# Requesting rows of delta * x eight units ahead of their use instead of ten

## The chip, the cores and the metric

The kernel runs as one program on 1 core of a Trainium2 chip. The metric is the device time of one execution in microseconds (us), given as a median over runs.

## The reference, cut to what matters

Four layers run one after another on images with 128 channels. Layers 0 and 1 each contain a selective scan over 4 batches, in four directions over 64 x 64 = 4096 positions; layer 0 has 128 channels there and layer 1 has 256. For every channel there are 16 states, and each is a first-order recurrence along the positions:

```python
def step(h, inp):
    d, u, b, c = inp
    dA = jnp.exp(d[..., None] * A)
    h = dA * h + (d * u)[..., None] * b[:, :, None, :]
    y = jnp.sum(h * c[:, :, None, :], axis=-1)
    return (h, y)
```

`d` is delta (a softplus of a projection), `u` the image x after a convolution, `b` and `c` are projections of x that all channels share. Around the scans stand 1x1 and 3x3 convolutions, norms and gates. Layer 2 is a message passing over 3x3 neighbours, layer 3 an attention over 7x7 windows; the change does not touch them.

## The kernel before

**Tiling.** The scans of layers 0 and 1 are 12 tasks: 4 batches with one tile of 128 channels for layer 0 and with two for layer 1. A task has 16 steps (4 directions, each in 4 pieces of 1024 positions), and a step has 16 units. A unit is 8 channels times 16 states on the 128 partitions, by 1024 positions. There are 3072 units, taken in pairs.

**A unit's way.** `prepare` computes for a whole step delta, delta * x and the projections. It stores delta * x to a DRAM tile `dud` (line 417, three of these tiles), cuts delta into three bfloat16 parts `parts`, copies these in 12 pieces of 64 KB into a tile `dp` (line 428), and asks for the rows of C, each repeated over 8 partitions, as `repC` (line 387). `load` (line 445) then requests for a unit its 8 rows of delta * x, each repeated over 16 partitions: 512 KB from `dud` into half of a pair tile `h` (line 453). There are nine pair tiles. VectorE multiplies the pair by B in place (`times`, line 459). TensorE spreads delta over the states and ScalarE takes the exponential (`decay`, lines 467 and 469) in one of two PSUM tiles `da`. VectorE runs the recurrence along the positions (`scan`, line 478), again in place. GpSimd (POOL) multiplies the pair by C (`times`, line 459), and TensorE adds up the states into `yps` (`add_up`, line 559). After that the pair tile can be filled again.

**Order.** The order is written by hand. `Scans.run` (line 587) goes through slots u, one per unit. In slot u VectorE gets the scan of unit u, in every other slot followed by the multiply by B of the next pair, TensorE the decay of unit u + 2 and, in odd slots, the sum of the pair whose last unit is u - 6. All DMAs of the scans are issued by SyncE (SP), in the order in which the program lists them; an entry that waits holds up all behind it. Tile frees and landings are told by semaphores, and eight of these serve the DMAs in turn, so that a DMA also waits for the eighth before it to land.

**What shares SyncE's queue.** `Plan.post` keeps a store or a load back until a due time that a planner computes, and `Plan.flush` issues it at the start of a later slot. Where u + 28 is a multiple of 16 (slot 4 of every step), line 628 issues all that is left of the preparing chains "prep" and "rep" and starts the preparation of another step; for a second channel tile this reads `xd` back (line 380). When `load` comes to the first unit of a step it flushes the chain "prep" (line 448). `between` hands out pieces of the other work of layers 0 and 1 ("side work": convolutions, norms, output projections), with loads such as `pad` (line 806), `x` (line 784) and `big` (line 1088) and stores (line 760). At the very end of a slot stands

```python
if 0 <= u + LEAD < total:
    self.load(u + LEAD)
```

so that all entries of slot u come before the request of unit u + LEAD.

Of the kernel before, what the change touches and what calls it, by code (L numbers as in the profile page):

```python
# [280 lines left out]
NU = ND * NSTEP * NG  # L281
FULL = 3600
AHEAD = 28
LEAD = 10
LAG = 5


class Scans:
# [298 lines left out]
    def run(self, between, head):  # L587
# [9 lines left out]
        for u in range(-12, total + LAG + 1):  # L597
# [52 lines left out]
            self.fill(self.plan.cells)  # L650
            if 0 <= u + LEAD < total:
                self.load(u + LEAD)
        while self.later:
# [1328 lines left out]
class Attention:  # L1982


    NH, HD, LEAD = 4, 32, 2

# [217 lines left out]
    def run(self):  # L2204
# [7 lines left out]
        def chunk_of(m):  # L2212
            return divmod(m, NCH)

        for m in range(self.LEAD):
            for piece in self.project(*chunk_of(m)):
# [6 lines left out]
        for n in range(total + 4):  # L2223
            if n % 4 == 0 and n < total:
                assert not pieces
                m = n // 4 + self.LEAD
                self.load(*chunk_of(m + 2))
# [243 lines left out]
```

## Time and profile before

| what | value |
|---|---|
| median of 3 runs | 12899.53 us (12898.79 to 12918.31) |
| the profiled execution, its own time | 12904.32 us |
| its span, first to last instruction | 12902.2 us |
| VectorE (DVE) busy | 11778.0 us, 91% |
| GpSimd (POOL) busy | 9663.1 us, 75% |
| TensorE (PE) busy | 9366.9 us, 73% |
| ScalarE (ACT) busy | 7769.0 us, 60% |
| requests of delta * x (`h<-dud`) | 3072 of 512 KB |
| bytes moved by DMA | 2463.66 MB, 191 GB/s over the span |
| scans, from about 112 us to 10,991 us | then layers 2 and 3 |

In the profile a line names the kernel's line (L478), the engine and operation, the tiles as output<-inputs, then busy time and the mean of one instruction in ns, then the idle time of the engine just before, and what ended it. In a timeline the first column is the start, the second the duration, and brackets hold the idle time before. In the list of waits stand the waiting engine and line, what it waited for, the total in us, how often, and the longest. "SPq" is SyncE's queue: its entries there are DMA issues, not the transfers themselves, which land later.

### The profile page before, as it was taken

To read this page: it belongs to the slowest core of one execution; us is meant where nothing else is said; L and a number is where in the kernel's file an instruction comes from. 1 tells how busy PE (TensorE), PEld (TensorE's weight loads), DVE (VectorE), ACT (ScalarE), POOL (GpSimd) and SP (SyncE) were. 2 spreads that over 40 slices of the span, in tenths; PEclk is the share of its full clock that TensorE was granted. 3 is DMA by queue.
4 is the path that set the end of the run, shared out by engine and by line. 5 is a ranking of instruction groups with operands and counts; after the bars stand their busy time and mean duration, and the time that the engine had idled before them with its cause. 6 is when DMAs were issued, how large, how long until landed. Compare 5 with 4: busy or idle time off the path is not lost. (4 is left out here: it accounts for less than half of the span.)

```text
span 12902.2 us, 128082 instructions
## 1 busy us (share of the span) xinstructions
PE 9366.9 (73%) x40881; PEld 2741.6 (21%) x41435; DVE 11778.0 (91%) x7219; ACT 7769.0 (60%) x10392; POOL 9663.1 (75%) x3167
## 2 busy tenths in 40 slices
PE   6777777767767767667777677776777776776799
PEld 1111111111111111111111111211112121221455
DVE  7999999999999989998999999999999999498666
ACT  4666656655666546655666555555555555476576
POOL 6888888887888778887888788888888888266200
PEclk8888899889889888998999899989899889887899
DMA  6888888898888978898888987778878777255200
GB/s 177 213 221 233 223 213 225 213 233 216 211 222 208 218 192 212 217 230 215 213 218 216 220 217 201 208 199 200 218 193 200 206 195 188 69 144 134 68 21 17
DMA packets 873450, 2463.66 MB, mean 191 GB/s; under 512 B 141888, under 2 KB 163528, under 8 KB 865096
## 3 DMA queue, kind: packets, MB, share of 16 engines
q1 hardware_dynamic: 872775, 2455.44, 74.3%
q8 instruction: 330, 5.41, 0.2%
q14 instruction: 345, 2.82, 0.1%
HBM read 2035.79 MB, written 268.17 MB: 179 GB/s over the span
## 5 line engine op out<-in xcount | busy, mean ns | idle before, releaser
L459 POOL TENSOR_TENSOR h<-h,repC 128x2048 f32<-128x2048 f32 x1536 | 6953.9, 4533 | 1476.3 <-ACT state L496 1176.7
L478 DVE TENSOR_TENSOR_SCAN h<-da,state,h 128x1024 f32<-128x1024 f32 x2304 | 5294.1, 2338 | 281.5 <-ACT da L469 168.1
L469 ACT ACTIVATE da<-da,av 128x1024 f32<-128x1024 f32 x3072 | 3327.5, 1087 | 2912.7 <-PE da L467 2486.2
L467 PE MATMUL da<-dp,spread 128*128 128x512 bf16 x5802 | 1995.7, 424 | 2441.2 <-DVE h L478 2398.5
L459 DVE TENSOR_TENSOR h<-h,B 128x2048 f32<-128x2048 f32 x1536 | 3476.6, 2263 | 173.1 <-issue 80.7
L559 PE MATMUL yps<-h,gather 128*32 128x512 f32 x12288 | 1866.7, 683 | 19.2 <-issue 4.5
L478 DVE TENSOR_TENSOR_SCAN h<-da,h 128x1024 f32<-128x1024 f32 x768 | 1719.4, 2278 | 66.0 <-ACT da L469 27.2
L467 PEld LDWEIGHTS <-spread 128*128 128x128 bf16 x6144 | 588.9, 101 | 4511.5 <-issue 4115.0
L565 PE MATMUL yps<-ones,nothing 128*128 128x512 bf16 x4197 | 1235.9, 404 | 37.3 <-issue 33.8
L102 ACT ACT_TABLE_LOAD x580 | 744.1, 1283 | 11.7 <-DMA x<-in_x_dram 1.7
L102 ACT CAST parts<-delta 128x1024 bf16<-128x1024 f32 x384 | 400.7, 1043 | 555.6 <-POOL delta L102 521.3
L102 POOL TENSOR_TENSOR delta<-delta,low 128x1024 f32<-128x1024 f32 x192 | 451.6, 2352 | 271.1 <-ACT low L102 220.4
L565 PEld LDWEIGHTS <-nothing 128*128 128x128 bf16 x4409 | 382.7, 101 | 1221.9 <-issue 929.4
L2175 POOL COPY wide_total<-total 128x128 f32<-128x128 f32 x128 | 37.4, 293 | 781.3 <-DVE total L2173 214.7
L102 PE MATMUL ms<-d,wts 128*128 128x512 f32 (+3 forms) x832 | 481.6, 691 | 164.5 <-POOL d L102 58.3
L102 PE MATMUL ms<-xd,xpdt 64*128 64x512 f32 x768 | 476.5, 703 | 107.4 <-ACT delta L102 25.3
L102 POOL TENSOR_TENSOR low<-delta,xc 128x1024 f32<-128x1024 f32 x192 | 502.9, 2619 | 9.1
L2144 ACT ACTIVATE s<-s,least 128x512 f32<-128x512 f32 x512 | 368.4, 720 | 232.6 <-DVE least L2131 228.7
L542 PE MATMUL yps<-y,ident 128*128 128x512 f32 x576 | 498.6, 955 | 4.3 <-ACT y L577 1.2
L1801 POOL TENSOR_TENSOR acc<-acc,part 128x1024 f32<-128x1024 f32 x120 | 301.9, 2519 | 195.7 <-DVE part L1795 195.7
L102 ACT ACTIVATE low<-ms,av 128x512 f32<-128x512 f32 x384 | 263.7, 687 | 287.7 <-PE ms L102 258.9
L102 POOL TENSOR_TENSOR parts<-delta,parts 128x1024 bf16<-128x1024 f32 x192 | 409.5, 2133 | 31.9 <-ACT parts L102 21.6
(295 smaller groups left out, 11050.8 us busy)
## 6 DMA issues: line engine op xcount, KB each, us to landing
h<-dud SPq DMA_DIRECT2D x3072, 512.0 KB
dp<-parts SPq DMA_DIRECT2D x2304, 64.0 KB
repC<-xdd SPq DMA_DIRECT2D x192, 512.0 KB
dud<-low SPq DMA_DIRECT2D x192, 512.0 KB
spread<-gd SPq DMA_DIRECT2D x72, 1024.0 KB
pad<-xid SPq DMA_DIRECT2D x176, 256.0 KB
x<-x SPq DMA_DIRECT2D x104, 256.0 KB
yd<-y SPq DMA_DIRECT2D x96, 256.0 KB
```

The lines of the kernel that those rows point to most:

```text
L102: return call(*args, **kw)
L459: engine.tensor_mul(pair, pair, t.prepared[step][name].unsqueeze(1).to_broadcast([P, 2, TS]))
L467: self.nc.tensor.matmul(da[:, cols], self.C.spread[:, jj, :], dp[:, j, cols], start=True, stop=True)
L469: self.nc.scalar.activation(da, da, AF.Exp, scale=t.W.a[:, at : at + 1])
L478: nc.vector.tensor_tensor_scan(h[:, way], da[:, way], h[:, way], 0.0 if step % NSTEP == 0 else t.states[step - 1][:, u % NG : u % NG + 1], ...
L542: self.nc.tensor.matmul(self.like_part(yps, k), self.C.ident, self.part(t.y, k, c, b), start=True, stop=False)
L559: self.nc.tensor.matmul(out, self.C.gather[jj], rhs, start=False, stop=jj == 3)
L565: self.nc.tensor.matmul(self.live["yps"], self.C.nothing, self.C.ones16, start=False, stop=False, skip_group_check=True)
L1801: (nc.vector if alone and pair else nc.gpsimd).tensor_add(acc, acc, part)
L2144: self.nc.scalar.activation(s, s, AF.Exp, scale=-1.0, bias=self.live["least", n][:, h : h + 1], accum_out=self.live["total", n][:, h : h + 1],
L2175: nc.gpsimd.tensor_copy(wide, total.unsqueeze(2).to_broadcast([P, self.NH, self.HD]))
```

## The change

One constant is altered: the request of unit x is listed at the end of slot x - 8 instead of slot x - 10. The nine pair tiles, all instructions and all other constants stay as they are. The first request moves from slot -10 to slot -8. Every entry of SyncE's queue that is not such a request moves ahead of two of them. The flush on line 448 takes place in slot 8 of a step instead of slot 6.

```diff
 FULL = 3600
 AHEAD = 28
-LEAD = 10
+LEAD = 8
 LAG = 5
```

## The prediction

> **What bounds the kernel now.** I read the head and the slices of the page first, then its costliest groups.
>
> ```profile
> PE 9366.9 (73%) x40881; PEld 2741.6 (21%) x41435; DVE 11778.0 (91%) x7219; ACT 7769.0 (60%) x10392; POOL 9663.1 (75%) x3167
> DVE  7999999999999989998999999999999999498666
> ...
> L478 DVE TENSOR_TENSOR_SCAN h<-da,state,h 128x1024 f32<-128x1024 f32 x2304 | 5294.1, 2338 | 281.5 <-ACT da L469 168.1
> L459 DVE TENSOR_TENSOR h<-h,B 128x2048 f32<-128x2048 f32 x1536 | 3476.6, 2263 | 173.1 <-issue 80.7
> ...
> L478 DVE TENSOR_TENSOR_SCAN h<-da,h 128x1024 f32<-128x1024 f32 x768 | 1719.4, 2278 | 66.0 <-ACT da L469 27.2
> ```
>
> VectorE is busy in nine tenths or more of nearly every slice up to about 11,000 us: that stretch is the scans, and there each pair of units costs it one multiply by B and two scans. Two starts of that multiply are 6.87 us apart at the median, so a unit takes 3.44 us. Nothing in the change shortens an instruction of VectorE. What can move is its idle time, 281.5 + 173.1 + 66.0 = 520.5 us in these three groups, and new idle time of the same kind.
>
> The change touches SyncE's queue, so next its own waits and two stretches of its timeline, an easy one and a crowded one.
>
> ```profile
> SPq L453 <- PE yps L559: 3154.9, 801, 19.7
> SPq L417 <- POOL low L102: 522.9, 135, 8.1
> SPq L453 <- DMA h<-dud: 403.4, 281, 3.7
> SPq L428 <- DMA h<-dud: 299.2, 239, 2.7
> ```
> ```profile
> 9553.07 0.51 SPq L387 DMA_DIRECT2D repC<-xdd  x1
> 9553.63 9.06 SPq L428 DMA_DIRECT2D dp<-parts  x12
> 9562.86 1.20 SPq L453 DMA_DIRECT2D h<-dud  x2
> ```
> ```profile
> 2954.61 13.41 SPq L428 DMA_DIRECT2D dp<-parts  x10
> ...
> 2972.63 3.51 SPq L806 DMA_DIRECT2D pad<-ld  x4
> 2976.18 7.21 SPq L453 DMA_DIRECT2D h<-dud  x4
> ```
> ```profile
> 2978.62 4.59 DVE L478 TENSOR_TENSOR_SCAN h<-da,state,h 128x1024 f32<-128x1024 f32 x2
> 2994.29 2.29 DVE L459 TENSOR_TENSOR h<-h,B 128x2048 f32<-128x2048 f32 x1 [11.07 <-issue]
> ```
>
> First: in the scans SyncE mostly waits for TensorE to let go of an old pair (`yps` is the sum that reads it last). Second: once per step a burst of small transfers stands between two requests. Third and fourth: where side work puts four `pad` loads into the same place, the request issued at 2976.18 landed at 2994.21 by its landing mark, and VectorE stood still for 11.07 us. The line says "issue"; the landing 0.08 us before the start says what it was.
>
> **The change part by part.**
>
> *Removed and added instructions: none.* 3072 requests, nine pairs, all other work stay. The sum holds moves only.
>
> *When the tiles come free: no change.* A pair is free once the sum over the pair nine before it has been issued, in slot x - 11 for an even unit x, and that is 10 units before VectorE wants it. In the trace the request follows this release by 0.1 us at the median for units 4, 6, 8, 10 and 12 of a step, issued about 32 us before the multiply that reads it. With a lead of ten the request's place in the queue (slot x - 10) is right behind its release; with eight it is two slots later. Where nothing else is queued in these two slots, SyncE still waits for the same release, and nothing moves: cost 0, covered by that wait. If the cover were gone, it would be two slots, 6.87 us, per request.
>
> *What is moved: every other entry now goes ahead of two more requests.* The heaviest case is the burst in slot 4 of each step, all of it there because line 628 flushes it: 12 `dp` parts, `repC`, and `xd` for the second channel tile. It stood between units 13 and 14; it will stand between 11 and 12. The burst lasts 13.6 us at the median (9.5 to 18.3 from the 10th to the 90th percentile), mostly waiting for POOL and for the eighth transfer before it. Its end is 9.9 us after the release of unit 14, hence some 17 us after that of unit 12. So units 12 and 13, now asked for 32.5 and 31.4 us ahead, will be asked for about 22.5 - 6.9 = 16 us ahead, units 14 and 15 directly behind them.
>
> *Is 16 us enough?* I took, for each request, issue, last landing mark and the start of the multiply that reads it. Landing takes 7.5 us at the median, 14.9 at the 95th percentile, over 15 in 148 cases of 3072. Here the Trainium skill has a rule, "SBUF — State Buffer", section "The DMA setup-cost knee": about 2 us fixed plus the bytes over 436 GB/s. That would be an estimated 3.2 us for these 512 KB, and 16 us would be plenty: cost 0. The trace disagrees: the fastest request takes 4.2 us, requests in a full queue land 2.1 us apart, and with eight outstanding one waits for seven before it. I use the trace.
>
> The margin between landing and use is 21.4 us at the median of all requests, 17.6 and 14.9 for units 14 and 15. A usual step therefore stays covered: units 12 and 13 keep about 9 us. The tail does not. Taking the smallest margin of each step from its pair 14-15 to pair 12-13 of the next step, 18 of 191 are under 2.9 us, 24 under 5 and 34 under 6.9, bunched where side work loads `pad` tiles.
>
> *The price of a late step.* The first request behind an entry is needed 6.87 us earlier than its counterpart now. Against that, two requests of 2.1 us no longer lie ahead of it: in a saturated queue the margin shrinks by 6.87 - 4.1 = 2.8 us. Where SyncE instead waits for the burst's sources and nothing is gained but two issues of 0.6 us, it shrinks by 5.7; by all of 6.87 where not even that. Summing (shrinkage - margin) over the steps below it gives 43 us at 2.9, 64 at 4, 86 at 5 and 140 at 6.9. The steps that are late at present are saturated ones, the others nearer the middle: I take 4.5, so about +75 us. Of that cost 11 steps pay on top of what they stall now. Behind a late multiply stand the pair's two scans on VectorE, and behind these TensorE's next decays (both PSUM tiles are taken) and POOL's multiply by C; all shift together, so a stall is paid once and not again downstream.
>
> *What gets better.* Entries other than requests come up to two slots earlier. Following VectorE's longest idle times back, seven go to such transfers and not to a request: loads of `x` (6.2 and 21.8 us), of `xpdt` (12.7), `big` (9.6) and `pad` (8.5 and 12.2), and a store of `dud` that held up ACT (15.0); 86 us in all. Two requests fewer ahead are 4 us each, -28 us; at most 6.87 each, -48. At least 0, where what is late was issued late for its own source.
>
> *Order of the `xdd` stores.* `load` flushes the preparing chain when it reaches a step's first unit: slot 6 now, slot 8 then. 150 such stores stand in slot 6. Two slots more let ACT finish `xd` first (SyncE waited 85.5 us there, 29 times). Their reader, `repC`, comes most of a step later. I take 0; the ends are -10 (fewer blocked requests) and +5 us.
>
> *The head.* The first request comes in slot -8 instead of -10, behind the same `dud` store. VectorE's first multiply waited for B on TensorE, with its request landed 3 us before: 0 to +5 us; I take 0.
>
> Sum: +75 - 28 = +47 us. The profiled execution took 12904.3 us around its span of 12902.2, 5 us above the median of 12899.5; its trace is used for differences only. 12899.5 + 47 = 12946.5, said as 12947.
>
> **The rivals.**
>
> *Hidden anyway.* SyncE's main wait is for free tiles, and the usual margin is over 14 us. If late steps and earlier side loads cancel (each about 45 us), the time stays at 12,880 to 12,920. Against it: the margins of 24 steps are under 5 us. Chance 0.16.
>
> *Faster.* The wait of 3154.9 us holds everything behind it, and a lead of eight lets side loads and stores pass. If the seven idle times shrink by 6.87 us each and late steps lose only 2.8, partly taken up by the idle time that follows them anyway, it is -48 and some +20: 12,870. It decides if the side transfers gain more than the requests lose. For it: 86 us hang on such transfers, only 29 us at present on late requests. Against it: side work is planned with its own landing times and rarely ends a wait of VectorE, while a request is waited for directly. Chance 0.14.
>
> *Late in many steps.* If the burst ends no earlier and four requests back to back land as slowly as now under load, steps with a pair 14-15 margin below 10 us count: 42 of 192, 219 us, less 28: 13,090. For it: the median 17 us after release. Against it: the median landing of 7.5 us. Chance 0.08.
>
> **How the numbers follow.** My forecast has 0.62, centred on 12947. A measurement of this kernel can tell about 0.2%, 26 us, from no change. Slower by more: 0.62 + 0.08 = 0.70; within: 0.16; faster: 0.14. The range goes from 12,865 (gains at their upper end) to 13,050 (shrinkage of 6.9 and some more), leaving about 0.2 outside. The likeliest case alone spans 12,920 to 13,020.
>
> **What would show it.** Right: three VectorE groups of the same length as before with idle time of the B multiply up from 173 to some 220 to 260 us, at multiplies of units 12 to 15 of a step with the landing just before the start; SyncE's wait for `yps` smaller than 3155 us; units 12 and 13 asked for some 16 us ahead. Wrong: idle time of the B multiply unchanged; or the scans' idle behind ACT down by more than the multiply's is up; or late requests spread over all units.

## The result: 12971.5 us, half a percent slower, and the profile after

| | before | after |
|---|---|---|
| median | 12899.16 us | 12971.52 us |
| ratio, 95% interval | | 1.005 [1.0038, 1.0062] |
| profiled execution | 12904.32 us | 12970.43 us |
| span | 12902.2 us | 12968.6 us |

A second set of runs of the changed kernel gave a ratio of 1.0054 [1.0041, 1.0066]. The change costs 66 to 72 us; 47 were forecast. The lines of the page that answer to those of before:

```profile
PE 9501.4 (73%) x41435; PEld 2751.4 (21%) x41435; DVE 11778.0 (91%) x7219; ACT 7772.9 (60%) x10392; POOL 9665.4 (75%) x3167
...
L478 DVE TENSOR_TENSOR_SCAN h<-da,state,h 128x1024 f32<-128x1024 f32 x2304 | 5293.1, 2337 | 267.0 <-ACT da L469 152.8
L459 DVE TENSOR_TENSOR h<-h,B 128x2048 f32<-128x2048 f32 x1536 | 3474.6, 2262 | 265.1 <-DMA h<-dud 110.3
L478 DVE TENSOR_TENSOR_SCAN h<-da,h 128x1024 f32<-128x1024 f32 x768 | 1719.1, 2278 | 56.8 <-ACT da L469 18.0
```

VectorE's busy time is the same to a tenth of a microsecond, and the means of these three instructions agree within 2 ns. What moved are the numbers behind the second bar, the idle times: the multiply by B waits 92.0 us more (173.1 to 265.1), and the main releaser is now a request, `DMA h<-dud`. The scans wait 23.7 us less. Together that is +68.3 us, against +66.4 us in the span. (TensorE's larger busy time is no extra work: 554 of its matmuls were missing from the first trace.)

SyncE's own waits for `repC`'s place, before the change:

```profile
SPq L387 <- POOL h L459: 187.5, 104, 4.5
```

After it, with two more:

```profile
SPq L453 <- PE yps L559: 1154.5, 347, 18.3
SPq L417 <- POOL low L102: 1008.3, 143, 11.8
SPq L387 <- POOL h L459: 688.7, 132, 10.9
```

The wait for a free pair tile fell from 3154.9 to 1154.5 us: the requests' place in the queue now binds more often than their tile. What SyncE gained it spends one entry further on: on POOL for `dud` (522.9 before) and on POOL for `repC` (187.5 before, 688.7 after), which heads the burst. So the burst did not come earlier. It began 4.1 us before the start of the scan of unit 4 at the median of the steps, and now begins 4.3 us before it; it ended 9.2 us after, and now 8.9. The requests, in turn, are issued nearer to their use at every unit of a step: the median margin between landing and use fell from 21.4 to 15.4 us, and the median landing time rose from 7.5 to 9.3 us.

The crowded stretch of the prediction, in the timelines of SyncE and VectorE after the change (start, duration, instruction, idle time before):

```profile
2955.88 15.04 SPq L428 DMA_DIRECT2D dp<-parts  x11
...
2975.49 3.49 SPq L806 DMA_DIRECT2D pad<-ld  x4
2979.02 4.63 SPq L453 DMA_DIRECT2D h<-dud  x3
```
```profile
2980.09 4.59 DVE L478 TENSOR_TENSOR_SCAN h<-da,state,h 128x1024 f32<-128x1024 f32 x2
2997.32 2.29 DVE L459 TENSOR_TENSOR h<-h,B 128x2048 f32<-128x2048 f32 x1 [12.64 <-issue]
```

The same block and the same four `pad` loads, the same kind of wait: 11.07 us became 12.64. But it was the multiply of units 14 and 15 before, and it is that of 12 and 13 now, one pair earlier. The page again says "issue"; the landing mark lies 0.08 us before the start.

A finer cut than any line gives: I count an idle time before a multiply by B as *late* where one of its two requests landed less than 0.3 us before it began. All tables below use this.

| idle time in us | late, all | at 12-13 | at 14-15 | at 0-11 | other, before B | before the scans |
|---|---|---|---|---|---|---|
| before | 28.6 | 0 | 27.6 | 0.9 | 144.6 | 347.4 |
| after | 140.8 | 87.7 | 31.7 | 21.5 | 124.3 | 323.8 |

Pairs whose request landed that late rose from 11 to 41 of 1536; before four of the 41 VectorE had no idle time.

### The profile page after: what moved, and what is told of

It reads as the page before. It is cut to its first block, busy times and chain, and to the rows that moved or that the text cites. A ratio compares the mean times of both kernels' runs of the same rounds, so it can differ in the third digit from the quotient of the medians.

```text
span 12968.6 us, 128662 instructions
## 1 busy us (share of the span) xinstructions
PE 9501.4 (73%) x41435; PEld 2751.4 (21%) x41435; DVE 11778.0 (91%) x7219; ACT 7772.9 (60%) x10392; POOL 9665.4 (75%) x3167
## 5 line engine op out<-in xcount | busy, mean ns | idle before, releaser
L467 PE MATMUL da<-dp,spread 128*128 128x512 bf16 x6144 | 2091.2, 426 | 2517.9 <-DVE h L478 2487.2
L459 DVE TENSOR_TENSOR h<-h,B 128x2048 f32<-128x2048 f32 x1536 | 3474.6, 2262 | 265.1 <-DMA h<-dud 110.3
L565 PE MATMUL yps<-ones,nothing 128*128 128x512 bf16 x4409 | 1293.5, 406 | 0.0
L559 PEld LDWEIGHTS yps<-h,gather 128*32 128x32 f32 x12288 | 257.9, 115 | 818.3 <-issue 695.4
```

The costliest lines, as they stand in the source:

```text
L459: engine.tensor_mul(pair, pair, t.prepared[step][name].unsqueeze(1).to_broadcast([P, 2, TS]))
L467: self.nc.tensor.matmul(da[:, cols], self.C.spread[:, jj, :], dp[:, j, cols], start=True, stop=True)
L559: self.nc.tensor.matmul(out, self.C.gather[jj], rhs, start=False, stop=jj == 3)
L565: self.nc.tensor.matmul(self.live["yps"], self.C.nothing, self.C.ones16, start=False, stop=False, skip_group_check=True)
```

## The experiments

Theory A was that a request is late where it stands behind the burst of slot 4. The first rival (B) was that two slots less are simply too short wherever side loads crowd the queue, whatever the request's place.

**The lead alone: nine.**

```diff
-LEAD = 10
+LEAD = 9
```


> Requests nine units ahead. Theory A (the burst in slot 4 of each step decides): unit 13, and with it the pair 12-13, already stands behind the burst, so most of the loss is there: VectorE's idle time before the multiply by B about 235 us (173 before, 265 with a lead of eight), time +40 to +55 us on before. Theory B (each slot of lead costs the same, wherever the request stands): half the loss, idle time about 219 us, time about +36 us.

Ratio 1.0011 [1.0003, 1.0019], about +14 us. Below both forecasts in time, yet the late idle time is 100.0 us, of which 40.8 at units 12-13 and 39.8 at 14-15. Waits before the scans fell to 311.1 us, other waits before B to 122.1, so VectorE's idle time rose by 13 us in all. The line before the multiply by B stands between 173.1 and 265.1:

```profile
L459 DVE TENSOR_TENSOR h<-h,B 128x2048 f32<-128x2048 f32 x1536 | 3475.7, 2263 | 222.1 <-issue 102.3
```

It follows that there are two terms, one lost and one won, and that they do not grow together: against the kernel before, late requests cost 71 us more at nine and 112 at eight, while the other idle times fell by 59 us and by 44. Neither theory alone gives +14.

**One pair of eight moved, the rest left.**

```diff
-            if 0 <= u + LEAD < total:
-                self.load(u + LEAD)
+            for x in range(u + 8, u + 11):
+                if 0 <= x < total and u == x - (8 if x % NG in (12, 13) else 10):
+                    self.load(x)
```


> Lead of ten, but units 12 and 13 of each step have a lead of eight, directly behind the burst; 14 and 15 follow them. Theory A: this alone brings the loss: idle time before the multiply by B 240 to 270 us, late at units 12 and 13; the scans' idle time behind ACT stays nearer to the 347 us of before than to the 324 us with a lead of eight, as side loads gain little; time +60 to +90 us. Theory B: one unit in eight is moved, idle time under 200 us, time under +25 us.

Ratio 1.0074 [1.0061, 1.0086], +95 us: more than the whole change. In its page:

```profile
L459 DVE TENSOR_TENSOR h<-h,B 128x2048 f32<-128x2048 f32 x1536 | 3476.5, 2263 | 300.1 <-DMA h<-dud 106.9
```

Late at units 12-13: 147.0 us, at 36 of the 192 pairs (four of them without idle time); at 14-15: nothing. The loss is reproduced with one unit in eight moved, and theory B, which allowed 25 us, falls. Theory A missed here too, in size: time and idle time lie above its ranges, and the waits before the scans fell to 329.3 us, near the 324 of the change, so most of that gain comes with this one pair as well. One reason may be the order. Slot 4 lists the requests of 12 and 14 and slot 5 those of 13 and 15, so 14 goes ahead of 13 here, which it does not in the change. Whether that explains the larger loss was not tested.

**The reverse: all moved, but 12 and 13 left.** The same loop with `10 if x % NG in (12, 13) else 8`.

> Lead of eight, but units 12 and 13 of each step keep a lead of ten, so they stand ahead of the burst as before and 14 and 15 behind it, as before. Theory A: idle time before the multiply by B back to 170 to 200 us, most of it not at units 12 and 13; time within 25 us of before. Theory B (two slots less for every request, too late wherever side loads crowd the queue): at most two units of eight are mended, idle time still 235 us or more, time +50 us or more.

Ratio 1.0013 [1.0006, 1.0019], +17 us; late at 12-13: 0. Theory A is right about the time. It is wrong on the idle time before B, 212.5 us instead of at most 200: the late ones moved on to units 14-15, 66.1 us against 27.6 before. These have a lead of eight here and follow other entries of slots 5 and 6 as well. So theory B keeps a share: behind the burst, two slots less cost late time also where the place relative to the burst stays.

**All pairs as soon as their tile is free.**

```diff
-            if 0 <= u + LEAD < total:
-                self.load(u + LEAD)
+            for x in range(u + 11, u + 13):
+                if u % 2 and 0 <= x < total:
+                    self.load(x)
```


> Both units of a pair requested in the slot in which their tile comes free: a lead of eleven for the even and twelve for the odd unit, so that 14 and 15 too stand ahead of the burst. Theory A: the late multiplies at units 14 and 15 (29 us in all before) go, idle time before the multiply by B about 145 us; side loads come later by up to two slots, scans' idle time 347 to 375 us; time -30 to 0 us. Rival (a queue that waits for free tiles holds up side loads and the burst more than it helps): +20 us or more, with more idle time behind ACT or at unit 0 of a step.

Ratio 0.9999 [0.9991, 1.0007]. No request is late at all, 0.0 us. All of it is given back before the scans:

```profile
L478 DVE TENSOR_TENSOR_SCAN h<-da,state,h 128x1024 f32<-128x1024 f32 x2304 | 5294.0, 2338 | 332.2 <-ACT da L469 219.5
L459 DVE TENSOR_TENSOR h<-h,B 128x2048 f32<-128x2048 f32 x1536 | 3476.0, 2263 | 146.0 <-issue 75.4
SPq L453 <- PE yps L559: 4435.7, 974, 18.7
```

281.5 became 332.2 us in the large group, and 347.4 became 400.8 in both, where theory A allowed 375. SyncE waits 4435.7 us for free tiles, and the burst starts 5.6 us later against VectorE's work than before. This is the change's mirror image: requests gain what the other entries lose.

**Only 14 and 15 ahead of the burst,** with a lead of ten for all others: in the loop `u == x - (x % NG - 3 if x % NG in (14, 15) else 10)`, over x from u + 10 to u + 12.

> Lead of ten, but units 14 and 15 of each step are requested in slot 3, directly ahead of the burst. Theory A (a request is late when it stands behind the burst; two places ahead of other entries cost those little): the multiplies late for their request go from 29 us to under 5, scans' idle time 347 to 375 us because the burst starts some 5 us later; time -30 to 0 us. Rival (the burst itself must not start later): scans' idle time up by 40 us or more as with all pairs requested at once (401 us), time the same as before or more.

Ratio 1.0005 [0.9997, 1.0013], no gain. Late multiplies fell to 9.8 us (under 5 was said), but the scans' idle time rose to 397.8 us, and the rival has it. Three of the new stalls are at unit 14 of steps with `pad` loads (7.3, 8.7 and 4.5 us), where TensorE waits for those loads; the stall behind a load of `x` grew from 6.2 to 11.9 us and that behind `xpdt` from 12.7 to 16.5.

**12 to 15 ahead of the burst, the others at eight or nine.** `u == x - (x % NG - 3 if x % NG in (12, 13, 14, 15) else 8)`, and the same with 9.

> Lead of eight, but units 12 to 15 of each step are requested by slot 3, all ahead of the burst. Theory A: late multiplies 15 to 25 us, all at units 0 to 3, scans' idle time 320 to 345 us, other idle time before the multiply by B about 122 us; time -50 to -20 us on before, faster than before and after. Rival (a lead of eight is short for the other units also, as a burst that starts later pushes them on): late multiplies 60 us or more, time +10 us or more.

> As the lead of eight with units 12 to 15 ahead of the burst, but with a lead of nine for the others. Theory A: late multiplies under 20 us, scans' idle time 311 to 340 us, time -55 to -25 us on before. Rival: as with units 12 to 15 alone at a lead of ten, no gain beyond the 29 us of late requests, or a loss through side loads, time -10 us or more.

Ratios 1.0022 [1.0015, 1.0028] and 1.0008 [1.0001, 1.0014]. Both expectations of a gain failed. The late idle time is 54.6 and 35.1 us, most of it at units 0 and 1 (39.6 and 33.3), and before the scans stand 385.0 and 391.4 us. A burst that starts later pushes on what comes after it.

**The pad loads.** The loads on line 806 are left out during the scans, once with a lead of eight and once with ten:

```diff
-        nc.sync.dma_start(out=pad[part, a - first : b - first, :], in_=image(src)[:, a:b, :])
+        if not nc.running:
+            nc.sync.dma_start(out=pad[part, a - first : b - first, :], in_=image(src)[:, a:b, :])
```


> Lead of eight, and the side work's loads of its padded tiles (pad, line 806) are left out during the scans, so its convolutions read what was there before; all else is done. Theory A with pads (late steps are those where pad loads meet the burst): late multiplies fall from 141 us to 20 to 50 us, the scans' idle time falls too as side work waits less; time 80 us or more under the kernel with a lead of eight. Rival (the burst alone is enough to make units 12 and 13 late): late multiplies stay over 100 us.

> Lead of ten, the side work's loads of its padded tiles left out during the scans (as in nopad8, which had a lead of eight and 9 us of late multiplies; its convolutions read what was there before). Theory A (burst and pad loads together make the loss): the lead hardly matters without them: late multiplies 0 to 3 us, scans' idle time 305 to 335 us, time within 20 us of nopad8. Rival (the burst costs by itself and the pads only added a level): at least 35 us faster than nopad8.

Ratios 0.9935 [0.992, 0.995] and 0.9927 [0.9912, 0.9942]: medians 12823.6 and 12811.7 us. Without these loads the lead of eight lies 10 to 12 us above the lead of ten, with overlapping intervals, and the idle times of the three groups add up to the same 436 us in both traces; with the loads it costs 66 to 72. Late: 9.3 us (8.9 at units 12-13) and 0.0. The multiply by B with a lead of eight, then of ten, both without the loads:

```profile
L459 DVE TENSOR_TENSOR h<-h,B 128x2048 f32<-128x2048 f32 x1536 | 3477.3, 2264 | 131.6 <-issue 63.9
L459 DVE TENSOR_TENSOR h<-h,B 128x2048 f32<-128x2048 f32 x1536 | 3474.9, 2262 | 116.8 <-issue 65.0
```

Of the 92 us that the change adds to this wait, 14.8 are left, and the scans wait 14.9 us less. So the burst takes the margin and the pad loads use up the rest: the burst alone makes little late. The loads left out are also 86 MB of the 2464 moved, so this does not tell whether it is their bytes or their places in the queue that count.

**The burst taken apart.** The twelve `dp` parts are issued one or two per slot in slots 4 to 12, in a chain of their own:

```diff
+        self.plan.flush("dp")
         parts = self.tile("parts", 1, shape=(P, 3, TS), dtype=BF16)
...
-            post("rep", lambda part=part, j=j: own(part, j), begin + (11 + 0.5 * i) * UNIT)
+            if self.plan.running:
+                self.plan.posted.append(("dp", begin + (16 + 0.7 * i) * UNIT, lambda part=part, j=j: own(part, j)))
+            else:
+                own(part, j)
```


> Lead of ten, the order of requests as before, but the twelve dp parts of a step are no longer issued as one burst in slot 4: one or two in each slot from 4 to 12, which is still ahead of their use from slot 14 on. repC stays in slot 3. Theory A (the burst as a block ahead of 14 and 15 makes them late, and nothing else has to be delayed for it to go): late multiplies from 29 us to under 10, scans' idle time within 20 us of 347, time -40 to -10 us. Rival (only bandwidth counts: the same bytes, so somebody else is late by as much): time within 10 us of before, or scans' idle time up by what the late multiplies fall.

> As above with a lead of eight. Theory A: units 12 and 13 no longer stand behind a block, late multiplies from 141 us to 15 to 60 us, what is left at steps with pad loads; time -30 to +20 us on before. Rival (pad loads and bandwidth alone): late multiplies 100 us or more, time +45 us or more.

With a lead of ten: ratio 1.0022 [1.0012, 1.0032]; with eight: 1.0002 [0.9994, 1.0011]. Late idle time falls to 1.2 and 30.9 us, as theory A has it (at units 12-13 with a lead of eight from 87.7 to 15.3), and the lead of eight no longer loses. The gain with ten does not come: 423.3 us stand before the scans, and both expectations for ten missed the time. Their cause is a new wait. ScalarE's next cast into the single `parts` tile has to wait until the last part has been copied out of it, and in crowded steps that is late:

```profile
6013.52 1.04 ACT L102 CAST parts<-delta 128x1024 bf16<-128x1024 f32 x1 [19.01 <-DMA dp<-parts]
```

Of the 18 stalls of VectorE over 4 us in this trace, behind the first multiply, twelve lead back to a wait of this cast for a DMA (eight by the name of `dp<-parts`, four where the trace names a request). With the burst apart, the lead of eight is the faster one, by 26 us between the medians (12937.8 and 12911.5): the sign of the change depends on what else stands in the queue.

**The changed kernel again,** beside these three.

> The changed kernel once more, beside the others: +55 to +80 us on before, late multiplies 120 to 160 us.

12974.4 us against 12908.8, late 150.9 us, 90.3 of it at units 12-13. As expected.

No version was measurably faster than the kernel before, apart from the two that leave work out.

## Why the prediction was right, and where its terms were off

**The place and the mechanism held.** Units 12 and 13 are now asked for 16.2 and 15.5 us ahead (about 16 was said) and keep a median margin of 11.3 and 8.3 us (about 9). A usual step is covered; the tail is not. The largest sum is at 12-13. Moving these units alone brings the loss, moving all others leaves +17 us, and with the block taken apart the same lead makes only 15.3 us late there: it is mainly their place behind the block. Elsewhere the wait for a free tile covers less than the prediction let it: units 4 to 10, put at "cost 0" where nothing else is queued, are asked for 1 to 4 us later at the median, and late idle time at units 0 to 11 rose from 0.9 to 21.5 us. The idle time before the multiply by B, 265.1 us, is just above the 220 to 260 that were to show the forecast right.

**The shrinkage was too small.** I took 4.5 us and got +75. The late idle time rose by 112 us (28.6 to 140.8). In the prediction's own sums over the margins that is a shrinkage of 6.0. At the medians the margin behind the burst shrank by 6.3 and 6.6 us (from 17.6 and 14.9 at units 14 and 15 to 11.3 and 8.3 at 12 and 13). The reason is in SyncE's waits: the burst hangs on POOL and keeps its place against VectorE's work within 0.3 us at the median, so nearly all of the 6.87 us is lost. I had seen in the trace that the burst waits for POOL, and still credited a saving.

**The gain was not made as I counted it.** I said -28 us from seven idle times. Before the scans 23.6 us went, and 20.3 from the waits before B that are not late requests. Of the seven, the stall behind `dud` fell from 11.4 to 3.6 us, and that behind `big` from 9.6 to 0.1. The line of `dud`:

```profile
4546.23 2.35 DVE L478 TENSOR_TENSOR_SCAN h<-da,state,h 128x1024 f32<-128x1024 f32 x1 [3.63 <-ACT da L469]
```

The one behind `x` at 720 us grew from 6.2 to 9.5, that of `xpdt` stayed (12.7, 12.8), as did the chain behind `x` at 4776 us. The two stalls behind `pad` at unit 0, 8.5 and 12.2 us, vanished only because late requests of units 12 to 15 now stop VectorE just ahead of them (9.4 us, and 6.9 with 8.4). There the idle time changed its name. The two fell to 0.9 us each, and these 18.8 us are most of the 20.3. Counted without them, the loss is about 93 us and the gain about 25. Part of the fall behind `big` is of this kind as well: after the change requests stop VectorE for 4.3 us at the multiply of the same pair and for 3.3 us three pairs before it.

**The head** does not belong to the gain. The first multiply began at 107.7 instead of 112.0 us, but VectorE's idle time before it rose from 30.1 to 31.2; with units 12 and 13, or 14 and 15, moved alone, where the first request keeps its lead of ten, it began at 106.5 and 107.1. So the lead of the first request does not explain these 4 us; their cause was not looked for.

The two misses went in opposite directions: +112 - 44 = +68 measured, +75 - 28 = +47 forecast. That the sum came as near as it did is in part luck.

**The order of the `xdd` stores** was expected to free SyncE from waiting for ACT. That wait rose from 85.5 to 179.7 us; no stall of VectorE was traced back to it. A likely reason can be read from the queue: 148 of the 256 stores stood in slot 6, and after the change 110 still do, issued by their due time ahead of two more requests, while 74 stand in slot 8.

**The rivals.** "Hidden anyway" would have needed the two terms to be equal; with a lead of nine, +71 against -59, they nearly are. "Faster" failed on its weighing: side entries did gain, but less than the requests lost. "Late in many steps" expected 42 steps at 5.2 us on average; there were 41 late pairs, in 34 steps, at 3.4 us.

## What to carry to other kernels

A request's lead counts from its place in the in-order queue, not from when its tile is free: look for what stands between, and when that can start at the earliest, before giving it a saving. When a fixed list of transfers is reordered, the margin that one class gains another loses; nine orders with the same work, the kernel before among them, had medians from 1 us below that kernel's to 29 us above it. Two lay outside, the change (+66 to 72 us) and the pair moved alone (+95): the two in which both units 12 and 13 stand with a lead of eight behind the whole block. Judge by the smallest margins, where two bursts meet, not by the median, and check that a stall is gone and has not only moved to the engine ahead.

## What the runs showed that I had not expected

With the same bytes and the burst spread out, requests that took over 15 us to land fell from 148 to 19 of 3072 (a lead of ten), and the median landing from 7.5 to 6.4 us. The `dp` parts are 64 KB each, 0.75 MB in a step beside the 8 MB of its requests, so their bytes alone do not explain it. I think that what they take is places: in the trace eight semaphores tell of the landings in turn, and no transfer is issued before the eighth before it has landed (SyncE waited 403.4 us for landings at line 453 before the change). Large transfers then pile up behind the block. That is argued from the order of the entries; it was not tried with another number of semaphores. Two things speak for care. Only eight of the 148 are of units 14 to 1, right behind the block; the others are of units 2 to 13, later in the row. And with the block whole and the pad loads left out there were 30. So block and pad loads make the slow landings together, and whether places or bytes count stays open.
